# Block 0 of the experts begun in attention's last steps, the third image routed two portions a step, row loads asked a step sooner

## The chip, the cores and the metric

The kernel runs on one core of a Trainium2 chip. The core has five engines that work side by side and wait for one another by semaphores: PE (matrix products into PSUM), DVE (vector work), ACT (activations, copies), POOL (here mostly a queue that issues indirect DMAs) and SP (a queue that issues DMAs). The metric is the device time of one execution in microseconds (us); lower is better. All times below are from one execution taken by the hardware profiler, counted from its first instruction, or from the three runs listed with it.

## What is computed

Two layers over 4 images of 32 x 32 tokens with 384 channels. Each layer is a token mixer and a feed-forward part, both with a residual and a layer norm ahead of it. Only the first layer bears on the change: an attention of 12 heads, and a mixture of 4 experts of which each token uses two.

```python
attn = softmax(q @ k.T * scale)                 # per image and head, 1024 x 1024
final = row[..., :, None] * col[..., None, :]   # from a choice of the 96 best tokens per group
attn = attn * final
attn = attn / (attn.sum(axis=2, keepdims=True) + 1e-08)
x = x + (attn @ v) @ proj_w.T

probs = softmax(ln(x) @ gate_w + gate_b)        # 4 experts, the best two are kept
h = gelu(ln(x) @ w1[e] + b1[e])                 # 384 -> 1536
y = h @ w2[e] + b2[e]                           # 1536 -> 384
x = x + sum over the two experts of weight * y
```

The second layer (a local attention called outlook, and a feed-forward part called kron) follows and is not touched.

## The kernel before

**Attention** (`attention`, L177) is one loop over 202 steps. A head takes 4 steps (`PAIRS`), an image 12 heads, so heads 0 to 47 fill steps 0 to 191; ten more steps empty the pipeline. PE, DVE, ACT and SP run in the order in which the Python code records their instructions; POOL's order is set by a scheduler that reckons when each instruction could start. In step s, in this order:

- PE makes the scores of step s (L649) into two PSUM buffers `ps_s`, and ACT turns them into exponentials `e` (L659);
- PE makes the head output `ps_o` of step s - 8 (`out`, L667 with `wv`) and the sums `ps_z` of step s - 1 (`total`, L667 with ones);
- at the first step of a head, `gather` (L678) sends the sums of the head before through memory: ACT copies them to `zr`, SP writes `z_row` (L683) and reads it back as `zz` (L685);
- at the last step of a head, `keep` copies its output (L731) and puts it into the image's `q` tile: SP writes one half of the keys' partial result (L740), POOL adds the other with an accumulating DMA (L738);
- the planner fits in parts of the next image's preparation, up to 2.6 us of PE work a step (`PACE`), and the search for the best tokens (`topk`, ACT L391, DVE L395 to L431);
- DVE multiplies two `e` tiles of step s - 7 by the reciprocal sums `rz` and adds them up (`share`, L711, about 1.27 us each), and makes `wv` (L718);
- at the second step of a head, `spread` (L690) adds up `zz` (L693), and SP writes the reciprocals as `r_row` (L697) and reads them back, spread over all partitions, as `rz` (L699);
- at the end of that same second step, `Head(n + 1)` is made: eight SP loads bring the next head's rows of q and k into `q4` and `k4` (L636, L637). The scores three steps later need them.

An image's tokens are routed one image later. `routed` (L793) is a generator; the step loop takes one portion of it per step, from the 27th step of the next image on. Its portions compute the gate, choose the two experts, count and place the tokens (`Router.route`, L1313), and scatter each token's line into a table in memory with 16 indirect DMAs on POOL (L1400). After the third image, image 2, its fifteenth portion computes `router.first()` (L1408): the rows of weights and tokens for the experts' first four blocks, `NFIRST`, which need only the first three images. The fourth image is projected and routed beside the experts' first blocks (`left`, L954, handed on as `beside`).

**Experts** (`experts`, L1573) work through 35 blocks of mostly 256 tokens. For block n, POOL fetches the up and down weights (L1603), the token list `ids` (L1617) and the tokens `xb` (L1627); two sets of buffers (`halves`) alternate. DVE normalises (`norm`, L1636), PE transposes (`turn`, L1646) and DVE copies out. Then PE makes 12 portions of up products, each 3 matmuls of 128 x 256 (L1723), each followed by a GELU on ACT (L1728), and the down products (L1747 in block 0, L1767 later). In block 0, after each of its last six up portions, a portion of `beside` projects one tile of image 3 (PE L306, DVE L782, output stored by SP at L787). Block 0's weights and tokens are recorded after attention's last step, but POOL's scheduler issues them earlier, as soon as their rows and their buffers are there.

Of the kernel before, what the change touches and what calls it, by code (L numbers as in the profile page):

```python
# [17 lines left out]
P = 128  # L18
# [158 lines left out]
def attention(net, outer, router, x, x1, unsafe, qkv_wT, gpT, proj_wT, proj_w, gate_w, gate_b):  # L177
# [24 lines left out]
    with ExitStack() as ctx:  # L202

        early = ctx.enter_context(tc.tile_pool(name="at_early", bufs=1))
# [416 lines left out]
        class Head:  # L621
            def __init__(self, n):
                self.n, self.b, self.h = n, n // NH, n % NH
                self.c, self.j = self.h // 4, self.h % 4
                self.rows = slice(32 * self.j, 32 * self.j + 32)
                self.im = images[self.b]
                assert (self.b, self.c, "qk") in reached

                self.q4 = big.tile([P, 512], FP, name="q4", tag="q4", bufs=2)
                self.k4 = big.tile([P, 512], FP, name="k4", tag="k4", bufs=2)  # L630
                q = self.im["q"][self.c][self.rows, :]
                k = self.im["k"][self.c][self.rows, :].rearrange("p (a e t) -> p a e t", e=2, t=P)
                for r in range(4):
                    rows_ = slice(32 * r, 32 * r + 32)
                    odd, half = divmod(r, 2)
                    nc.sync.dma_start(out=self.q4[rows_, :], in_=q[:, 512 * half : 512 * half + 512])  # L636
                    nc.sync.dma_start(  # L637
                        out=self.k4[rows_, :].rearrange("p (a t) -> p a t", t=P), in_=k[:, :, odd, :]
                    )
                self.es = []  # L640
                self.s = tiny.tile([P, NB], FP, name="s", tag="s")
# [36 lines left out]
            def gather(self):  # L678

                zr = work.tile([P, 512], FP, name="zr", tag="zr", bufs=1)  # L680
                nc.scalar.copy(zr, self.z)
                there = rows.tile([4, 512], FP, name="z_row", tag="z_row")
                nc.sync.dma_start(out=there, in_=zr.rearrange("(j r) q -> j r q", r=32)[:, 0, :])  # L683
                self.zz = tiny.tile([P, 2, NB], FP, name="zz", tag="zz", bufs=2)
                nc.sync.dma_start(  # L685
                    out=self.zz,
                    in_=there.rearrange("j q -> (j q)").rearrange("(e p i) -> p e i", e=2, p=P),
                )
# [180 lines left out]

        step = -100  # L870
# [16 lines left out]
        heads.append(Head(0))  # L887
        goal = spent
        for step in range(STEPS + OUT + 2):
# [9 lines left out]
            if u == 0 and 0 < n <= NHEAD:  # L899
                heads[n - 1].gather()  # L900
            if 0 <= step - OUT < STEPS:
                if (step - OUT) % PAIRS == PAIRS - 1:
                    heads[(step - OUT) // PAIRS].keep()
            b, i = divmod(step, PAIRS * NH)
# [11 lines left out]
            if b and o > 2 * NB:  # L916
                next(routing[b - 1], None)
# [14 lines left out]
            if u == 1 and n + 1 < NHEAD:  # L932
                heads.append(Head(n + 1))
# [30 lines left out]
    return left  # L964
# [276 lines left out]
class Router:  # L1241
# [10 lines left out]
    def __init__(self, net, pool, keep, psum):  # L1252
# [34 lines left out]
        self.all = None  # L1287
# [285 lines left out]
def experts(net, router, x1, x2, wup, wdown, beside):  # L1573
# [12 lines left out]
    with ExitStack() as ctx:  # L1586
# [4 lines left out]
        halves = [pool(f"ex_{n}", 1) for n in range(2)]  # L1591
# [3 lines left out]
        def rows(n):  # L1595
            w, t = router.firsts if n < NFIRST else router.all
            return w[:, n : n + 1], t[:, n : n + 1]

        def weights(n):
            up = halves[n % 2].tile([P, KC * HID + NF], FP, name="up", tag="up")  # L1600
            down = halves[n % 2].tile([P, NF * C + C], FP, name="down", tag="down")
            for t, w in ((up, wup), (down, wdown)):
                nc.gpsimd.indirect_dma_start(  # L1603
                    out=t, out_offset=None, in_=w,
                    in_offset=bass.IndirectOffsetOnAxis(ap=rows(n)[0], axis=0),
                )
            return up, down

        beside = beside(work)
        ids, xbs = {}, {}  # L1610

        def tiles(n):
            return 1 if NFIRST <= n < NLEAD else TT

        def tokens(n):
            t = ids[n] = halves[0].tile([P, TT, router.LINE], I32, name="ids", tag="ids", bufs=6)
            nc.gpsimd.indirect_dma_start(  # L1617
                out=t[:, : tiles(n), :].rearrange("p t w -> p (t w)"), out_offset=None,
                in_=net.table.rearrange("(r t) w -> r (t w)", t=tiles(n)),
                in_offset=bass.IndirectOffsetOnAxis(ap=rows(n)[1], axis=0),  # L1620
            )

        def fetch(n):
            xb = xbs[n] = halves[n % 2].tile([P, TT, C], FP, name="xb", tag="xb")
            last = (B - 1 if n < NFIRST else B) * NTOK
            for t in range(tiles(n)):
                nc.gpsimd.indirect_dma_start(  # L1627
                    out=xb[:, t, :], out_offset=None, in_=x1[:last, :],
                    in_offset=bass.IndirectOffsetOnAxis(ap=ids[n][:, t, 0:1], axis=0),
                )  # L1630

        def norm(n):
            xb = xbs[n]
            own = ids.pop(n).bitcast(FP)
            for t in range(tiles(n)):
                nc.vector.tensor_scalar(  # L1636
                    xb[:, t, :], xb[:, t, :], own[:, t, 1:2], own[:, t, 2:3], ALU.subtract, ALU.mult
                )

        def turn(n):  # L1640
            xb = xbs.pop(n)
            xbT = halves[n % 2].tile([P, KC, XB], FP, name="xbT", tag="xbT")
            for t in range(tiles(n)):
                ps = router.psum()
                for c in range(KC):
                    nc.tensor.transpose(ps[:, c * P : (c + 1) * P], xb[:, t, c * P : (c + 1) * P], net.ident)  # L1646
                nc.vector.tensor_copy(
                    xbT[:, :, t * P : (t + 1) * P], ps[:, :C].rearrange("p (c t) -> p c t", c=KC)
                )
            return xbT  # L1650
# [39 lines left out]
        ws = {0: weights(0)}  # L1690
        for n in range(NFIRST):
            tokens(n)
        fetch(0)
        norm(0)
        xbT = turn(0)
        for n in range(NXB):
# [6 lines left out]
            if n + 1 < NXB:  # L1703
                if n + 1 >= NFIRST:
                    tokens(n + 1)
                ws[n + 1] = weights(n + 1)
                fetch(n + 1)
# [5 lines left out]
            up, down = ws.pop(n)  # L1713
# [5 lines left out]
            for f in (*range(0, 3), *range(6, 9), *range(3, 6), *range(9, 12)):  # L1719
                ps = ps_h.tile([P, XB], FP, name="ps_h", tag="h")[:, :size]  # L1720
                for k in range(KC):
                    o = k * HID + f * P
                    nc.tensor.matmul(  # L1723
                        ps, lhsT=up[:, o : o + P], rhs=xbT[:, k, :size], start=k == 0, stop=k == KC - 1,
                    )
                if f % 3 == 0:
                    hs[f // 3] = hp.tile([P, 3, XB], FP, name="h", tag="h")
                nc.scalar.activation(  # L1728
                    hs[f // 3][:, f % 3, :size], ps, AF.Gelu, bias=up[:, KC * HID + f : KC * HID + f + 1]
                )  # L1730
                if NFIRST <= n < NLEAD or router.all is None and n < NFIRST - 1 and (n or f % 6 >= 3):
                    next(beside, None)
                if whole and f in (8, 11):
                    g = len(ss)
                    ss.append(paired(hs[g], hs[g + 2], g))
            if n + 1 < NXB:
                norm(n + 1)
            else:
                net.scale(0, added)
            out = net.yg[first_row(n) : first_row(n + 1), :].rearrange("(p t) c -> p t c", t=tiles(n))  # L1740
            if not whole:
                for t in range(tiles(n)):
                    if t == tiles(n) - 1 and n + 1 < NXB:
                        xbT = turn(n + 1)
                    ps = ps_y.tile([P, C], FP, name="ps_y", tag="y")
                    for f in range(NF):
                        nc.tensor.matmul(  # L1747
                            ps, lhsT=hs[f // 3][:, f % 3, t * P : (t + 1) * P], rhs=down[:, f * C : (f + 1) * C],
                            start=f == 0, stop=f == NF - 1,
                        )  # L1750
                    y = work.tile([P, C], FP, name=f"y{t}", tag=f"y{t}", bufs=2)
# [31 lines left out]
            if n + 1 < NXB:  # L1783
                xbT = turn(n + 1)
# [540 lines left out]
def metaformer_kernel(  # L2325
# [57 lines left out]
    with ExitStack() as outer:  # L2383
        router = routing(outer)
        eng = mybir.EngineType
        with tc.manual_schedule(engines={eng.PE, eng.DVE, eng.Activation, eng.SP}):
            left = attention(
                net, outer, router, x, x1, unsafe, qkv_wT, gpT, proj_wT, proj_w, gate_w, gate_b
            )
            done = experts(net, router, x1, x2, wup, wdown, left)  # L2390
# [75 lines left out]
```

## Time and profile before

| | us |
| --- | --- |
| three runs | 2771.51, 2778.27, 2787.73 (median 2778.27) |
| the profiled execution | 2779.0 |
| its span, first to last instruction | 2776.9 |
| PE busy | 2563.9 (92%) |
| DVE busy | 1746.2 (63%) |
| ACT busy | 1272.1 (46%) |
| POOL busy | 414.5 (15%) |
| last scores of attention start | 1194.7 |
| last `ps_o` of attention ends | 1226.5 |
| first up product of block 0 starts | 1229.6 |
| first up product of block 1 starts | 1279.7 |

From 200 to 300 us PE is busy 98.1 us of 100 and DVE 76.9; from 1158.7 to 1188.8, PE 17.9 of 30.1; from 1203.7 to 1226.6, PE 12.7 of 22.9 at a granted clock of 0.55, DVE 18.6. A line of the timeline holds the start, the duration of all that it merges, the engine, the source line, the operation, output and inputs, a count, and in brackets the idle time before it and what ended that. SPq stands for the queue of SP. "Slices" are fortieths of the span, 69.4 us each.

### The profile page before, as it was taken

The page shows a single profiled execution, that of the slowest core. Times are in us where ns is not written, and L with a number is a line of the kernel's source. Part 1 is how long each engine was busy: PE and PEld are TensorE (multiplying, and loading weights), DVE is VectorE, ACT ScalarE, POOL GpSimd, SP SyncE. Part 2 cuts the span into 40 slices and gives each one's busy share as a digit, 9 for nine tenths or more (in the row PEclk, how much of TensorE's full clock was granted, in tenths as well). Part 3 has the DMA queues.
Part 4 walks back from the last instruction along what each step waited for, and adds up shares of the span by engine and source line. Part 5 has one row for each costly group of instructions (what it writes and reads, how often), then busy time and mean ns, then how long its engine had stood idle before and what let it go on. Part 6 is the DMA issues. An engine that isn't in the chain of part 4 may idle for free. (4 is left out here: it accounts for less than half of the span.)

```text
span 2776.9 us, 40200 instructions
## 1 busy us (share of the span) xinstructions
PE 2563.9 (92%) x14667; PEld 1555.7 (56%) x14667; DVE 1746.2 (63%) x4490; ACT 1272.1 (46%) x2086; POOL 414.5 (15%) x501
## 2 busy tenths in 40 slices
PE   6879998989898999679999999999999998999988
PEld 3323332333332332137889999999999974555542
DVE  2367768777776778555635444455465457897962
ACT  3768776667676777421121211211211123445455
POOL 1000000020003000412221111222222111110000
PEclk9989999989998999779999999999999999999999
DMA  5133334322331233445475455556656626765532
GB/s 108 33 98 91 103 91 124 104 56 63 92 78 46 70 87 85 130 128 190 158 280 207 181 187 207 213 208 222 228 195 223 225 100 220 213 213 180 174 117 93
DMA packets 215807, 404.13 MB, mean 146 GB/s; under 512 B 83345, under 2 KB 176849, under 8 KB 202545
## 3 DMA queue, kind: packets, MB, share of 16 engines
q0 software_dynamic: 26960, 209.05, 21.9%
q1 hardware_dynamic: 178928, 181.52, 21.8%
q10 hardware_dynamic: 9712, 10.91, 1.3%
q8 instruction: 118, 1.93, 0.3%
q14 instruction: 89, 0.72, 0.1%
HBM read 304.34 MB, written 49.00 MB: 127 GB/s over the span
## 5 line engine op out<-in xcount | busy, mean ns | idle before, releaser
L1728 ACT ACTIVATE h<-ps_h,up 128x256 f32<-128x256 f32 (+1 forms) x420 | 194.9, 465 | 835.2 <-PE ps_h L1723 818.6
L1723 PE MATMUL ps_h<-xbT,up 128*128 128x256 f32 (+1 forms) x2520 | 531.2, 371 | 2.5 <-ACT h L1728 1.4
L1723 PEld LDWEIGHTS ps_h<-xbT,up 128*128 128x128 f32 x2520 | 462.4, 191 | 64.9 <-ACT h L1728 2.2
L711 DVE CUSTOM_DVE_ANT_0 e<-e,rz,inv 128x1024 f32<-128x1024 f32 x384 | 475.2, 1274 | 35.7 <-DMA rz<-r_row 35.7
L659 ACT ACTIVATE e<-ps_s,ten 128x1024 f32<-128x1024 f32 x384 | 407.6, 1107 | 96.5 <-PE ps_s L649 41.6
L649 PE MATMUL ps_s<-q,k 32*128 32x512 f32 x1536 | 291.3, 669 | 66.1 <-ACT e L659 32.7
L667 PE MATMUL ps_o<-e,wv 128*32 128x512 f32 x1536 | 229.0, 671 | 47.6 <-DVE wv L718 30.2
L738 POOL DMA_DIRECT2D q<-po x96 | 76.0, 874 | 977.9 <-DMA q<-po 651.1
L667 PE MATMUL ps_z<-e,rt_ones 128*32 128x512 f32 x1536 | 219.7, 646 | 0.0
L391 ACT ACTIVATE below<-tk_left,tk_bound 128x1024 bf16<-128x1024 f32 (+1 forms) x160 | 184.2, 1151 | 70.6 <-DVE tk_bound L397 60.1
L1767 PE MATMUL ps_y<-wsum,hsum 128*128 128x192 f32 x1116 | 197.1, 330 | 9.9 <-DVE hsum L1683 5.4
L649 PEld LDWEIGHTS ps_s<-q,k 32*128 32x128 f32 x1536 | 89.4, 191 | 203.2 <-issue 89.3
L1767 PEld LDWEIGHTS ps_y<-wsum,hsum 128*128 128x128 f32 x1116 | 183.3, 192 | 13.7 <-DVE y L1771 7.4
L1907 PE MATMUL ps_a<-wa,xnT 128*128 128x486 f32 x384 | 162.4, 572 | 1.8 <-ACT xnT L174 1.8
L1771 DVE TENSOR_TENSOR y<-ps_y,y 128x192 f32<-128x192 f32 x155 | 55.4, 357 | 167.8 <-PE ps_y L1767 162.0
L667 PEld LDWEIGHTS ps_o<-e,wv 128*32 128x32 f32 x1536 | 31.7, 112 | 209.0 <-issue 83.5
L306 PE MATMUL ps_t<-xnT,wqkv 128*128 128x512 f32 x288 | 136.9, 616 | 3.3 <-ACT xnT L488 2.6
L1567 POOL DMA_INDIRECT yt<-yg,index x64 | 78.0, 1218 | 358.8 <-DVE x L1870 164.7
L667 PEld LDWEIGHTS ps_z<-e,rt_ones 128*32 128x32 f32 x1536 | 52.8, 118 | 132.7 <-issue 129.7
L1767 PE MATMUL ps_y<-down,h 128*128 128x192 f32 x744 | 126.0, 326 | 0.0
L1767 PEld LDWEIGHTS ps_y<-down,h 128*128 128x128 f32 x744 | 122.6, 190 | 1.6
L1907 PEld LDWEIGHTS ps_a<-wa,xnT 128*128 128x128 f32 x384 | 71.2, 189 | 74.2 <-issue 70.2
(403 smaller groups left out, 3588.1 us busy)
## 6 DMA issues: line engine op xcount, KB each, us to landing
band<-room SPq DMA_DIRECT2D x32, 1560.0 KB
rz<-r_row SPq DMA_DIRECT2D x48, 512.0 KB
yg<-y SPq DMA_DIRECT2D x67, 192.0 KB
q<-q SPq DMA_DIRECT2D x192, 64.0 KB
k<-k SPq DMA_DIRECT2D x192, 64.0 KB
room<-none SPq DMA_DIRECT2D x64, 192.0 KB
x<-x SPq DMA_DIRECT2D x34, 192.0 KB
o<-in_x_dram SPq DMA_DIRECT2D x33, 192.0 KB
```

Of the source, the lines that this page charges most:

```text
L306: nc.tensor.matmul(ps, lhsT=lhsT(k), rhs=rhs(k), start=k == 0, stop=k == KC - 1)
L391: nc.scalar.activation(junk[:n], left[:n], AF.Sign, bias=bound[:n], accum_out=over[:n])
L649: nc.tensor.matmul(ps[:, half * 512 : half * 512 + 512], lhsT=self.k4[r, u * P : (u + 1) * P], rhs=self.q4[r, :], start=True, stop=True,)
L659: nc.scalar.activation(e, ps, AF.Exp, bias=shift, scale=QK_SCALE)
L667: nc.tensor.matmul(ps[r : r + 32, :], lhsT=lhsT(odd), rhs=self.es[2 * u + odd][:, half * 512 : half * 512 + 512], start=u == 0, stop=u == ...
L711: nc.vector.tensor_tensor_reduce(self.es[m], self.es[m], self.rz, 1.0, self.im["inv"][:, m, self.h : self.h + 1], ALU.mult, ALU.add, self. ...
L738: nc.gpsimd.dma_start(out=there, in_=po[r : r + 32, :], accum_op=ALU.add)
L1567: self.nc.gpsimd.indirect_dma_start(out=y, out_offset=None, in_=self.net.yg[: first_row(self.complete(i // NB)), :], in_offset=bass.Indire ...
L1723: nc.tensor.matmul(ps, lhsT=up[:, o : o + P], rhs=xbT[:, k, :size], start=k == 0, stop=k == KC - 1,)
L1728: nc.scalar.activation(hs[f // 3][:, f % 3, :size], ps, AF.Gelu, bias=up[:, KC * HID + f : KC * HID + f + 1])
L1767: nc.tensor.matmul(ps, lhsT=left[f], rhs=right[:, f, :], start=f == 0, stop=f == HF - 1)
L1907: nc.tensor.matmul(pa[:, :HW_], lhsT=xnTs[i][:, k, :], rhs=wa[:, k, hh * HW_ : (hh + 1) * HW_], start=k == 0, stop=k == KC - 1,)
```

## The change

There are four parts.

1. `Head(n + 1)` is made at the first step of head n instead of the end of its second, and its loads become a generator, `load`. `gather` issues three of the eight between its two own DMAs; the rest follow it in the same step, ahead of `spread`'s.
2. Of image 2 the loop takes two routing portions a step.
3. As soon as `router.first()` has run, the pool of attention's early tiles (weights, the image's transposed tokens, moved to the other side of the memory for it) is closed, and the first half's buffers of the experts take its place. Block 0's up weights and the token lists of four blocks are asked for in that step, its tokens one step later, its down weights three steps after those; its norm stands in step 188 and its transposes in step 189, copied out by ACT instead of DVE. In steps 192 to 199 its 12 up portions are made, by turns one and two a step, into the score buffers, and the GELU results go into three free `q` tiles.
4. In `experts`, block 0 then starts at its down products. The six portions of `beside` that stood between its up products stand after every fourth down portion. The helpers of `experts` become the methods of a class `Blocks`, the same for all later blocks. The norm of block 1 is recorded after block 0's up portions as before, which now means ahead of all six portions of `beside`.

```diff
-        early = ctx.enter_context(tc.tile_pool(name="at_early", bufs=1))
+        soon = ctx.enter_context(ExitStack())
+        early = soon.enter_context(tc.tile_pool(name="at_early", bufs=1, side="right"))
...
+            def load(self):
...
                     nc.sync.dma_start(out=self.q4[rows_, :], in_=q[:, 512 * half : 512 * half + 512])
+                    yield
                     nc.sync.dma_start(
                         out=self.k4[rows_, :].rearrange("p (a t) -> p a t", t=P), in_=k[:, :, odd, :]
                     )
+                    yield
...
-            def gather(self):
+            def gather(self, loads):
...
                 nc.sync.dma_start(out=there, in_=zr.rearrange("(j r) q -> j r q", r=32)[:, 0, :])
+                for _ in range(3):
+                    next(loads, None)
...
+        def chunks():
+
+            cols, h = [], None
+            for f in range(NF):
+                if f % 4 == 0:
+                    h = lasting.tile([P, NTOK], FP, name="q", tag="q", bufs=6)
+                if f % 2 == 0:
+                    ps = ps_s.tile([P, NTOK], FP, name="ps_s", tag="s")
+                p = ps[:, f % 2 * 512 : f % 2 * 512 + XB]
+                blocks.up(0, f, blocks.xbT, p, XB)
+                col = h[:, f % 4 * XB : f % 4 * XB + XB]
+                blocks.gelu(0, f, p, col)
+                cols.append(col)
+                yield
+            blocks.cols = cols
...
-            if u == 0 and 0 < n <= NHEAD:
-                heads[n - 1].gather()
+            if u == 0 and n <= NHEAD:
+                loads = iter(())
+                if n + 1 < NHEAD:
+                    heads.append(Head(n + 1))
+                    loads = heads[-1].load()
+                if n:
+                    heads[n - 1].gather(loads)
+                for _ in loads:
+                    pass
...
+            if step >= STEPS:
+                if step == STEPS:
+                    upward = chunks()
+                for _ in range(1 + step % 2):
+                    next(upward, None)
...
-                next(routing[b - 1], None)
+                for _ in range(2 if b == B - 1 else 1):
+                    next(routing[b - 1], None)
+            if blocks is None and router.firsts is not None:
+                assert pending == [None, None] and begun == len(tiles)
+                soon.close()
+                pool = outer.enter_context(tc.tile_pool(name="ex_0", bufs=1, side="right", reuse_waits="tile"))
+                blocks = Blocks(net, router, x1, wup, wdown, pool)
+                known = step
+                blocks.weigh(0, 0)
+                for one in range(NFIRST):
+                    blocks.tokens(one)
+            if blocks and step == known + 1:
+                blocks.fetch(0)
+            if blocks and step == known + 4:
+                blocks.weigh(0, 1)
+            if step == STEPS - 4:
+                blocks.norm(0)
+            if step == STEPS - 3:
+                blocks.xbT = blocks.turn(0, nc.scalar.copy)
...
-            if u == 1 and n + 1 < NHEAD:
-                heads.append(Head(n + 1))
...
+            early = n == 0 and blocks.cols is not None
-            for f in (*range(0, 3), *range(6, 9), *range(3, 6), *range(9, 12)):
+            for f in () if early else (*range(0, 3), *range(6, 9), *range(3, 6), *range(9, 12)):
...
             if n + 1 < NXB:
-                norm(n + 1)
+                blocks.norm(n + 1)
...
                     for f in range(NF):
+                        h = blocks.cols[f] if early else hs[f // 3][:, f % 3, :]
                         nc.tensor.matmul(
-                            ps, lhsT=hs[f // 3][:, f % 3, t * P : (t + 1) * P], rhs=down[:, f * C : (f + 1) * C],
+                            ps, lhsT=h[:, t * P : (t + 1) * P], rhs=down[:, f * C : (f + 1) * C],
                             start=f == 0, stop=f == NF - 1,
                         )
+                        if early and f % 4 == 3:
+                            next(beside, None)
```

The new methods that the step loop calls:

```python
def weigh(self, n, part):
    name, w = (("up", self.wup), ("down", self.wdown))[part]
    t = self.halves[n % 2].tile([P, w.shape[-1]], FP, name=name, tag=name)
    self.ws.setdefault(n, []).append(t)
    self.nc.gpsimd.indirect_dma_start(
        out=t, out_offset=None, in_=w,
        in_offset=bass.IndirectOffsetOnAxis(ap=self.rows(n)[0], axis=0),
    )
def up(self, n, f, xbT, ps, size):
    up = self.ws[n][0]
    for k in range(KC):
        o = k * HID + f * P
        self.nc.tensor.matmul(
            ps, lhsT=up[:, o : o + P], rhs=xbT[:, k, :size], start=k == 0, stop=k == KC - 1,
        )
def gelu(self, n, f, ps, out):
    up = self.ws[n][0]
    self.nc.scalar.activation(out, ps, AF.Gelu, bias=up[:, KC * HID + f : KC * HID + f + 1])
```

## The prediction

> **What bounds the kernel now.** I first read the busy shares by slice, which show where PE stops being full, then PE's timeline over that place, then SP's and POOL's timelines over the same stretch, and last the list of waits from 60 to 1240 us, for the part of the change that touches every head. Times are us in the profiled execution.
>
> ```profile
> PE   6879998989898999679999999999999998999988
> PEclk9989999989998999779999999999999999999999
> ```
>
> PE (and its granted clock) is at 9 tenths almost everywhere, except in slices 17 and 18, 1111 to 1250 us: attention's last steps and the start of the experts. Work moved into that hole is nearly free; work moved elsewhere is not.
>
> ```profile
> 1167.38 1.04 PE L667 MATMUL ps_z<-e,rt_ones 128*32 128x512 f32 x8
> 1180.11 4.37 PE L649 MATMUL ps_s<-q,k 32*128 32x512 f32 x8 [11.69 <-DMA q<-q]
> ...
> 1224.59 1.94 PE L667 MATMUL ps_o<-e,wv 128*32 128x512 f32 x8 [1.00 <-DVE wv L718]
> ...
> 1229.62 11.16 PE L1723 MATMUL ps_h<-xbT,up 128*128 128x256 f32 x42 [0.65 <-DVE xbT L1647]
> 1240.63 2.12 PE L306 MATMUL ps_t<-wproj,q 128*128 128x388 f32 x6
> ...
> 1279.68 1.46 PE L1723 MATMUL ps_h<-xbT,up 128*128 128x256 f32 x6
> ```
>
> PE's timeline has three parts. One stall of 11.7 us waits for the last head's row loads. Then a tail, to 1226.5, waits for DVE (wv) at every step. Then block 0: from the last out, 1226.53, to the first up product of block 1, 1279.68, are 53.2 us.
>
> ```profile
> 1163.23 0.32 SPq L697 DMA_DIRECT2D r_row<-rr  x1
> 1173.92 0.32 SPq L699 DMA_DIRECT2D rz<-r_row  x1
> 1174.33 0.55 SPq L636 DMA_DIRECT2D q<-q  x1
> ```
>
> SP's queue tells the stall's cause. rz is issued only when r_row has landed, normally 1.4 us later; here 10.7 us. The row loads stand behind it.
>
> ```profile
> 1160.32 1.96 POOL L1603 DMA_INDIRECT up<-in_wup_dram,rows_w_first  x1 [0.30 <-issue]
> 1162.58 0.97 POOL L1603 DMA_INDIRECT down<-in_wdown_dram,rows_w_first  x1 [0.30 <-issue]
> ...
> 1177.44 0.94 POOL L1627 DMA_INDIRECT xb<-x,ids  x1 [8.52 <-DMA ids<-table,rows_t_first]
> ```
>
> POOL had just asked for block 0's weights: 128 x 4620 and 128 x 4992 floats, 2.37 + 2.56 = 4.92 MB. A 4 KB row issued into that burst landed at its end, and so did ids. 4.92 MB in the 11.6 us from 1162.3 to 1173.9 is 424 GB/s: 5.6 us for up, 6.0 for down.
>
> ```profile
> DVE e L711 <- DMA rz<-r_row: 35.7, 15, 13.2
> DVE zall L693 <- DMA zz<-z_row: 35.4, 19, 4.1
> PE ps_s L649 <- DMA k<-k: 11.0, 10, 4.2
> ```
>
> The waits (total, times, longest) show what the earlier row loads touch: 11.0 us of PE waiting for k rows can go; DVE's waits for zz and rz can grow.
>
> **A, the row loads a step sooner.** No load is added; eight per head move in SP's order. Now: z_row, zz (median 1.7 us after z_row, when it has landed), r_row (at +3.85 when DVE is prompt), rz (+5.3), then eight loads of 0.52 to 0.65 us. After: z_row, three loads, zz, five loads, r_row, rz. Three loads and z_row's own 0.53 make zz +2.4, 0.7 later. With zz's 0.4 and five loads r_row comes no sooner than +6.2, up to 2.35 later. I set this against each head's own slack, the start of its first share (DVE L711) less rz's landing, taken as issue + 3.8, as in the two last heads, where DVE waited for it. Over the 46 heads that load rows behind them the excess is 22 us of new DVE waiting, in 21 heads; zz adds 0.7 at each of its 19 waits, 13 more. PE mostly takes a wv some time after it is ready (0 to 4.7 us; under 1 us in two heads of five). Taking that margin off head by head leaves 8 to 9 us of the 22, and I take 4 of the 13: a loss of 12. The gain: 11.0 us of PE waits go, and the half-speed restarts after the two longest of them (4.45 and 3.50 us for eight rows against 2.3) give 3 more: 14. A = -2, with ends -14 (every delay covered) and +21 (all 35 lost, 14 gained). The order of the next image's preparation shifts by a step in some places, with the same instructions; its cover is the planner's spread, and I price it at nothing.
>
> **B, image 2 (the third) routed two portions a step.** The fifteenth portion, which gives block 0's rows, falls in step 178 instead of 185. Its DVE work moves (matmul portion 3.0, copies 0.4, rows 5.1, from 1120.9 to 1124.0 and 1153.8 to 1159.0) and is not added: DVE is busy 18 of 20 us around 1100, so steps 171 to 178 lengthen by about what 179 to 185 lose. The 16 scatters (POOL L1400, 1.27 us each, 25 us with their stretches) start near step 176 instead of 181. In the changed program's POOL order up, four ids, down follow them directly: although the source asks for down four steps later, nothing it waits for holds it back. So the burst stays about 12 us, near steps 180 to 183 of head 44's chain, and up and down are split only by five issues (some 6 us). What is late next is z_row, zz, r_row or rz of that head: four transfers in turn, each at most one half (6 us) late, needed some 11.5 us after z_row. The last head's rows are by then not behind rz. I count 6.5 us of new stall for the 13.2 now at 1166, plus a slow restart less (4.37 against 2.3): about -7.5. Ends: -16, if the burst falls between two chains, and -2, if it hits two links fully.
>
> The Trainium skill speaks against this picture: "DMA: Bandwidth & Descriptors", section Queues, rings and completion order, has each DMA engine alternate between queues packet by packet, so a small SP transfer should get its turn inside POOL's burst. The 10.7 us row says it waited for the whole of it. By the rule alone the stall would not be this burst's, nothing of the 7.5 would be gained, and the forecast would be about 7 us higher; the row decides.
>
> **C, block 0's up products in the tail.** Moved: 36 up matmuls (72 rows, 15.70 us in a later block, 1.31 for each of 12 portions), 12 GELUs of 465 ns and their table load (1.28). In steps 192 to 199 DVE works 2.94 us a step (two L711, d, wv), which sets the pace; PE's out is 1.06 at full clock, and 1 or 2 portions add 1.3 or 2.6, 3.0 a step on average: covered, but only at full clock (granted now: 0.55), which the added work itself should bring. If it doesn't, PE sets the pace, 5.8 a step. DVE's norm of block 0 (0.87) and PE's six transposes with ACT's two copies (0.9 and about 1.1) go into steps 188 and 189, where PE is nearly full: D = +1.5, ends 0 and +3.
>
> From the last out (t = 0), PE does: two portions, 2.6; four down portions, 8 of 24 rows of 7.90, to 5.2; project 0 needs head 47's rows in q: ACT's copy 0.6, SP's issue 0.6, POOL's accumulate 2.0 behind that (1180.6 + 0.6 to 1183.2 for head 44), 0.8 to issue and 2 to land: 6, so project 0 ends at 8.1; four portions, 10.7; project 1, 12.8; four portions, 15.5. Project 2 needs the PSUM buffer of project 0, emptied by a DVE add that now stands behind DVE's norm of block 1. That needs xb of block 1, which in POOL's order stands behind up of block 2, up and down of block 1: 7.28 MB, 17.2 us from about 5, then 0.4 MB and its landing: 24. Norm 0.87 and add 0.7: 25.5. Project 2 at a cold clock 3.0; transposes with their waits 1.5; three times four portions and a project, 14.2: block 1 begins near 44. 53.2 - 44 = 9 gained, of 15.7 + 3.4 that left. Ends: -19 (xb in time, no stall) and -5 (accumulated rows and x loads late too). Weights of block 1 land near 22: covered by 22 us.
>
> **Sum.** Profiled time 2779.0 (span 2776.9 and 2.1 around it; the runs' median is 2778.27). -2 - 7.5 - 9 + 1.5 = -17: 2762.
>
> **Rivals.** (1) The burst misses head chains and xb lands in time: 2779 - 2 - 16 - 19 + 1.5 = 2743.5. For it: the burst is shorter than a head's 21 us; against: the FIFO-like wait of ids (8.52) at 1177. (2) The stall only moves: B -2, C -5, A 0, D +1.5 gives 2773.5. For it: down follows up directly, and xb follows 7.28 MB; against: the last rows no longer wait behind rz. (3) Slower: r_row behind five loads in 46 heads, the full 35 us in DVE's path with the k waits replaced by it: 2779 + 35 - 7.5 - 9 + 1.5 = 2799. It decides once A costs more than 15 + 14 = 29. For it: slack under 0.8 in twenty of the 46 heads; against: PE is busy 90 of 100 us from 100 to 1085, DVE 72, so part of a DVE wait is always covered.
>
> **How the numbers follow.** Chances: the likeliest (2754 to 2770) 0.45, rival 1 0.22, rival 2 0.22, rival 3 0.11. The range reaches into both sides: 2742 to 2788. Half a per cent, 13.9 us, is about what the measurement can tell from no change, so faster means under 2764.4: rival 1, two thirds of the likeliest and a little of rival 2, 0.54; slower means over 2792, 0.11; the rest 0.35.
>
> **What would show it.** A: k-row waits of PE near nothing; the zz and rz waits of DVE grown by 10 to 35. B: up issued near 1135, no wait of 11 us before the last head's scores, but a DVE wait of 3 to 9 for zz or rz one head after the burst begins. C: L1723's successor in the tail at a clock near 1, DVE shares still 2.94 apart, then one PE wait of about 10 us before project 2, behind DVE's norm of block 1, and 44 us from last out to block 1. Wrong would be: shares further apart than 3.1, DVE waiting at block 0's norm for xb, or a main part (100 to 1085) longer by over 15 us.

## The result, and the profile after

| | before | after |
| --- | --- | --- |
| median of 6 runs each, us | 2777.74 | 2813.36 (2809.45 to 2818.41) |
| ratio | 1 | 1.0143, 95% interval 1.0121 to 1.0166 |
| span of the profiled execution, us | 2776.9 | 2813.9 |

The change made the kernel slower, by 36 us between the medians and 37 between the profiled spans; the interval is 1.2 to 1.7%. The forecast was 2762 and its range ended at 2788. The third rival (slower, 2799) named the mechanism and was still 14 us short.

The busy shares of PE by slice, of the changed kernel (a slice is now 70.3 us):

```profile
PE   6879898889998998687999999999999998999988
```

The hole, now in slices 17 to 19, is still there. But slices 5 to 16, attention's main part, have digits that add up to 102 where they added up to 104: the loss is spread thin, and a page of slices hardly shows it. The starts of single instructions do. How much later than in the profile before a head's `z_row` is issued by SP, and what follows attention:

| place | head 6 | 12 | 18 | 24 | 36 | 42 | 44 | 46 | last out ends | block 1 starts | block 4 starts | end |
| --- | --- | --- | --- | --- | --- | --- | --- | --- | --- | --- | --- | --- |
| later by, us | 8.1 | 15.0 | 21.1 | 26.3 | 26.9 | 38.8 | 58.9 | 38.9 | 40.9 | 36.1 | 37.6 | 37.0 |

By head 41 (37.4), before image 2's routing and block 0's weights come into play, the whole loss is there. It doesn't grow evenly: from head 24 to head 37 it stays between 21 and 27. Image 2's routing costs 20 and gives 20 back; the tail and block 0 give back a few.

The waits of the changed kernel from 60 to 1240 us (total, times, longest):

```profile
DVE e L719 <- DMA rz<-r_row: 78.1, 32, 5.7
DVE zall L701 <- DMA zz<-z_row: 59.1, 28, 4.2
```

PE's waits for k rows are gone from the list, as forecast (step A's gain came). The waits for rz and zz have grown from 35.7 and 35.4 to 78.1 and 59.1: by 66, not by the 35 that A allowed at most. SP's queue shows why. One head (33) before, then after:

```profile
902.49 0.54 SPq L683 DMA_DIRECT2D z_row<-zr  x1
904.21 0.37 SPq L685 DMA_DIRECT2D zz<-z_row  x1
906.90 0.33 SPq L697 DMA_DIRECT2D r_row<-rr  x1
908.31 0.32 SPq L699 DMA_DIRECT2D rz<-r_row  x1
```

```profile
923.42 0.54 SPq L689 DMA_DIRECT2D z_row<-zr  x1
...
925.95 0.59 SPq L693 DMA_DIRECT2D zz<-z_row  x1
926.58 0.63 SPq L644 DMA_DIRECT2D k<-k  x1
...
929.21 0.63 SPq L644 DMA_DIRECT2D k<-k  x1
929.95 0.53 SPq L705 DMA_DIRECT2D r_row<-rr  x1
931.58 0.33 SPq L707 DMA_DIRECT2D rz<-r_row  x1
```

r_row goes out 6.5 us after z_row instead of 4.4, and rz 8.2 instead of 5.8. This is one of the better heads: over heads 0 to 45 the medians after z_row are 2.55 (zz), 7.88 (r_row) and 9.91 (rz), against 1.72, 4.38 and 6.09 in a second profile of the kernel before, taken below (e0). In 33 of the 46 heads the first share starts within 0.6 us of rz's landing (its issue + 3.8); in e0 it is 15. The row loads have turned the chain z_row, zz, r_row, rz from a frequent limit into the usual one.

The tail and block 0, from PE's timeline of the changed kernel, and the DVE instruction that the long wait stands for:

```profile
1266.40 1.06 PE L673 MATMUL ps_o<-e,wv 128*32 128x512 f32 x8
...
1274.34 2.12 PE L307 MATMUL ps_t<-wproj,q 128*128 128x388 f32 x6
...
1278.87 2.12 PE L307 MATMUL ps_t<-wproj,q 128*128 128x388 f32 x6
...
1296.33 4.22 PE L307 MATMUL ps_t<-wproj,q 128*128 128x388 f32 x6 [12.76 <-DVE gate_o L791]
...
1315.73 1.46 PE L1711 MATMUL ps_h<-xbT,up 128*128 128x256 f32 x6
```

```profile
1294.69 0.96 DVE L1683 TENSOR_SCALAR xb<-xb,ids 128x384 f32<-128x384 f32 x2 [23.12 <-DMA xb<-x,ids]
```

Two projections run at once; the third waits 12.8 us because DVE stands at block 1's norm, which waits 23 us for xb. The forecast was 10, with the same cause. From the last out to block 1 it takes 48.3 us (forecast 44).

### The profile page after: what moved, and what is told of

Same layout as the page of the kernel before. It is cut to its first block, busy times and chain, and to the rows that moved or that the text cites. A ratio compares the mean times of both kernels' runs of the same rounds, so it can differ in the third digit from the quotient of the medians.

```text
span 2813.9 us, 40158 instructions
## 1 busy us (share of the span) xinstructions
PE 2566.9 (91%) x14667; PEld 1553.0 (55%) x14667; DVE 1746.1 (62%) x4488; ACT 1275.0 (45%) x2088; POOL 411.7 (15%) x501
## 3 DMA queue, kind: packets, MB, share of 16 engines
q8 instruction: 118, 1.93, 0.3%
## 5 line engine op out<-in xcount | busy, mean ns | idle before, releaser
L1711 PE MATMUL ps_h<-xbT,up 128*128 128x256 f32 (+1 forms) x2448 | 512.7, 370 | 2.4 <-ACT h L1717 2.4
L1711 PEld LDWEIGHTS ps_h<-xbT,up 128*128 128x128 f32 x2448 | 447.5, 190 | 61.0 <-ACT h L1717 3.6
L655 PE MATMUL ps_s<-q,k 32*128 32x512 f32 x1536 | 284.0, 682 | 50.2 <-ACT e L665 44.1
```

What stands on the lines that cost most here:

```text
L655: nc.tensor.matmul(ps[:, half * 512 : half * 512 + 512], lhsT=self.k4[r, u * P : (u + 1) * P], rhs=self.q4[r, :], start=True, stop=True,)
L1711: self.nc.tensor.matmul(ps, lhsT=up[:, o : o + P], rhs=xbT[:, k, :size], start=k == 0, stop=k == KC - 1,)
```

## The experiments

e1 to e4 ran on one chip, e0 and e6 to e8 on a second, e5, e10 and e11 on a third, each group with the kernel before beside it. The chips differ (before: 2748.87 on the first, 2778 on the two others), so ratios are compared. "Loads" are a head's eight row loads.

**e1: the loads put back**, all else as changed.

```diff
-                loads = iter(())
-                if n + 1 < NHEAD:
-                    heads.append(Head(n + 1))
-                    loads = heads[-1].load()
...
             search()
+            if u == 1 and n + 1 < NHEAD:
+                heads.append(Head(n + 1))
+                for _ in heads[-1].load():
+                    pass
```

> The changed kernel with the eight row loads put back behind rz, where the kernel before has them; the earlier block, the double routing and the up products in the tail stay. Theory A (SP's order: r_row and rz stand behind the loads in every head): the 37 us that the steps up to 172 lost come back and the 5 us won behind the last out stay, about 2772, between 2766 and 2780, and r_row is again 3.8 us after z_row. Rival (the main part is longer because of something else in the change, such as the pools' new places or the burst): still above 2800.

Measured: ratio 1.0020 (1.0007 to 1.0033), 5.5 us (1.9 to 9.1) above the kernel before. The main part's loss is gone: r_row's median is 4.29 again, and DVE's waits (60 to 1240 us) are near those of the kernel before:

```profile
DVE zall L701 <- DMA zz<-z_row: 41.5, 21, 3.8
DVE e L719 <- DMA rz<-r_row: 33.2, 16, 9.1
```

But with the three other parts of the change, forecast at -15 together, the kernel is not faster than before, and the ratio lies just above the expected range (2780 beside 2778 is 1.001).

**e2: the loads alone**, in the kernel before: the same edit as in the change, nothing of its other parts.

> The kernel before with the row loads alone asked a step sooner, as in the changed kernel. Theory A: slower by 30 to 42, 2808 to 2820, less some 10 if the last head's 11.7 us wait for its rows goes with it. Rival (something else in the change): within 8 of the kernel before.

Measured: 1.0139 (1.0122 to 1.0156), 38 us (34 to 43). The waits are those of the changed kernel, and more:

```profile
DVE e L718 <- DMA rz<-r_row: 93.3, 34, 15.3
DVE zall L700 <- DMA zz<-z_row: 59.7, 32, 4.3
```

One part of the change, by itself, is as slow as the whole. e1 and e2 together show that the loads' place in SP's queue is the cause of the loss, and exclude the pools and the burst as its cause.

**e3 and e4: which link?** e3 issues three loads between z_row and zz and five behind rz. e4 issues none ahead of zz and eight between zz and r_row.

```diff
                     heads[n - 1].gather(loads)
-                for _ in loads:
-                    pass
...
             search()
+            if u == 1:
+                for _ in loads:
+                    pass
```

The first edit is e3's, the second, in `gather`, e4's.

```diff
-                for _ in range(3):
-                    next(loads, None)
                 self.zz = tiny.tile([P, 2, NB], FP, name="zz", tag="zz", bufs=2)
```

> The changed kernel with three loads between z_row and zz, and five behind rz: zz is 0.7 to 0.9 us late as in the changed kernel, r_row is late only by that. If the delay of r_row and rz is what costs: 4 to 10 above the kernel with all loads put back, so 2776 to 2784. If the delay of zz costs as much, or if it is that rows are moved while z_row lands: above 2795.

> The changed kernel with no load ahead of zz, and all eight between zz and r_row: zz is prompt (1.7 us after z_row), r_row comes no sooner than 1.7 + 0.5 + 8 x 0.64 = 7.3 us after z_row, 8.6 with the two room stores. If the delay of r_row and rz is what costs: 2810 to 2825, as slow as the changed kernel or slower. If the delay of zz is what costs: below 2790.

Measured: e3 1.0051 (1.0034 to 1.0068), 6.6 us above e1; e4 1.0260 (1.0237 to 1.0283), 64 above e1 and well beyond the changed kernel. The waits of e3, then of e4 (60 to 1240 us):

```profile
DVE zall L701 <- DMA zz<-z_row: 69.9, 31, 4.3
DVE e L719 <- DMA rz<-r_row: 39.4, 21, 8.2
PE ps_s L655 <- DMA k<-k: 5.7, 2, 5.1
```

```profile
DVE e L717 <- DMA rz<-r_row: 130.5, 36, 13.3
DVE zall L699 <- DMA zz<-z_row: 35.9, 22, 3.6
```

In e3 zz is 0.9 later (median 2.61), rz only by that, and DVE waits for zz 28 us longer than in e1 (41.5); PE's k waits shrink from 19.4 to 5.7, and the sum of it is small. In e4 zz is prompt, rz goes out at 10.72, and DVE waits 97 us longer for it than in e1 (33.2). A delay that begins behind zz is enough to cost this much (e4); e3 costs less because its whole chain is only 0.9 late.

**e5: the room stores.** Attention's steps also issue stores (L85, `room`, 0.64 us each) between the loads and r_row; step A had left them out.

```diff
-            if zeros and step >= 4:
-                zeros.pop(0)()
...
                 heads[n - 1].spread()
+            if zeros and step >= 4:
+                zeros.pop(0)()
```

> The changed kernel with each step's two room stores (L85) issued behind r_row and rz instead of ahead of them; the loads stay a step sooner. If the prediction's r_row time (no sooner than +6.2) was missed mainly because two room stores of 0.64 us stand behind the five loads in the heads up to about 19: r_row 1.3 us sooner in those heads, and 8 to 20 us of the 38 come back: 1.007 to 1.011 of before. Rival (the loads alone do it, room is hidden): within 5 of the changed kernel, 1.0125 to 1.016.

Measured: 1.0133 (1.0114 to 1.0152), not told apart from the changed kernel. The edit did less than expected: SP's timeline shows that one of the two stores still stands ahead of r_row, whose median only fell from 7.88 to 7.17. So the omission explains part of why +6.2 was too early, but 0.7 of r_row's lateness bought no time that can be told apart. What both stores would bring wasn't tried.

**e0: the kernel before again**, for a second profile beside the next three.

> The kernel before, unchanged, for a profile on the same chip as the next three. Expected: the wait of 11 to 12 us for a row before the last heads' scores, and 49 to 53 us from the last out to block 1, wherever the chip's own time lies.

Measured: 2777.69, its span 2775.6. PE's list of waits from 60 to 1240 us:

```profile
PE ps_s L649 <- DMA k<-k: 20.4, 7, 11.8
```

The long wait is there again (11.8). But block 1 starts 48.8 us after the last out, not 53.2: in the profile on record DVE waited 8.3 us for one x row block (1.6 here), PE then waited 2.8 for DVE's norm of block 1, and 24 rows of down products after it took 9.6 instead of 7.9. This execution, e2 and e7 (48.8, 48.8, 48.7) have none of this.

**e6: the loads earlier still**, for head n + 2 at the end of head n's fourth step, when their buffers come free, ahead of z_row.

```diff
+            if u == PAIRS - 1 and n + 2 < NHEAD:
+                heads.append(Head(n + 2))
+                for _ in heads[-1].load():
+                    pass
```

> The changed kernel with the eight loads of head n+2 asked at the end of head n's fourth step, as soon as their buffers are free and ahead of the next z_row. Theory A: zz, r_row and rz are prompt again, PE's waits for k rows (11 us before) go too: 5 to 12 faster than the changed kernel with the loads put back, so 0.995 to 1.000 of the kernel before. Rival (SP's queue is simply full there: the loads wait for the scores and z_row comes behind 5.2 us of issue): z_row late by 1 to 3 in every head, 1.01 or more.

Measured: 1.0060 (1.0041 to 1.0078): slower, the rival's way, though less than its 1.01. ACT's copy, then SP's queue:

```profile
709.00 0.60 ACT L687 COPY zr<-ps_z 128x512 f32<-128x512 f32 x1
```

```profile
709.17 0.63 SPq L644 DMA_DIRECT2D k<-k  x1
709.91 0.54 SPq L689 DMA_DIRECT2D z_row<-zr  x1
```

zr was ready at 709.60, z_row went out at 709.91 behind the last load. On average over 48 heads z_row is issued 1.62 us after zr is ready; in e0 it is 0.06. The queue must be empty at the moment when z_row, zz, r_row and rz become ready, and here it isn't.

**e7: the double routing alone**, in the kernel before.

```diff
             if b and o > 2 * NB:
-                next(routing[b - 1], None)
+                for _ in range(2 if b == B - 1 else 1):
+                    next(routing[b - 1], None)
```

> The kernel before with the third image routed two portions a step, nothing else. By step B of the prediction: 2 to 16 faster, likeliest 7.5 (0.997). Rival (the burst meets another head's rows and DVE is full there): the burst starts some 35 us sooner, a wait of 8 to 12 for rows or rz stands there in place of the 11.7, and the time stays within 4 of before, or is above it.

Measured: 0.9979 (0.9958 to 1.0000), 5.8 us below before, 0 to 11.7. Against e0, z_row of heads 43, 44, 45 and 46 stands at +8.2, +15.7, +9.2 and -2.8, and the last out ends 2.7 sooner. The routing is moved, not saved; POOL asks for the weights at 1131.3 to 1133.5, between two heads' chains, and the 11.8 us wait for rows is gone from the list (the longest wait for zz in that stretch is 5.1). Yet at the last out only a quarter of it is left as a gain. ACT stands for 3.6, 1.8 and 3.0 us between 1129 and 1158 for no instruction or transfer that the profile names; what these are wasn't settled.

**e8: block 1's norm later**, e1 with norm and transposes of block 1 at the end of block 0's down portions.

```diff
-                blocks.norm(n + 1)
+                if not early:
+                    blocks.norm(n + 1)
...
                     for f in range(NF):
+                        if early and t == tiles(n) - 1 and f == 8:
+                            blocks.norm(n + 1)
...
+                if early:
+                    xbT = blocks.turn(n + 1)
```

> The changed kernel with the loads put back, and block 1's norm and transposes moved from the middle of block 0's down portions to their end. Theory (project 2 waits only because DVE stands at that norm for xb): the wait of 12.4 goes, block 1 starts 34 to 37 after the last out instead of 47, and the time is 10 to 13 below the kernel with the loads put back: 0.997 to 0.999 of before. Rival (the weights or x loads of block 1 come as late as xb): PE waits at block 1's first product instead, less than 4 gained.

Measured: 0.9973 (0.9959 to 0.9987), 7.5 below before. The wait before project 2 is gone, and block 1 starts 41.5 us after the last out (e1: 46.9), not 34 to 37. DVE's timeline shows the next limit, and SP's when the late transfer was asked for:

```profile
1253.26 0.55 DVE L790 TENSOR_TENSOR o<-o,ps_t 128x384 f32<-128x384 f32 x1 [12.11 <-DMA o<-in_x_dram]
```

```profile
1234.81 0.44 SPq L772 DMA_DIRECT2D o<-in_x_dram  x1
```

An x row block (192 KB) asked at 1234.81, 2 us after the last of three weight requests (1229.23 to 1232.76, 7.28 MB), was there at 1253.3; the profile's DMA records hold rows of these weights from 1231.5 to 1252.5. By the ratios e8 is 13 us below e1, as expected, but from the last out to block 4 it saves only 6; e1 ran on another chip, and the rest isn't explained.

**e10: the x rows ahead of the burst**, e8 with the seven o loads issued at the first projection, into seven buffers.

```diff
-                o = late[0].tile([P, C], FP, name="o", tag="o", bufs=2)
+                o = late[0].tile([P, C], FP, name="o", tag="o", bufs=7)
...
-            if t + 1 < NB:
-                residue(B - 1, t + 1)
+            for soon_ in range(1, NB) if t == 0 else ():
+                residue(B - 1, soon_)
```

> The kernel with the loads put back and block 1's norm moved to the end, and all seven remaining loads of x rows (o) asked at the first projection, into seven buffers instead of two. Theory (in that kernel DVE's 12.1 us wait for one o, asked 2 us behind the 7.28 MB of weights, has taken the place of the wait for xb): no DVE wait above 3 us between the last out and block 1, block 1 starts 35 to 38 after the last out instead of 41.5, 3 to 6 faster: about 0.995 of before. Rival (the o loads only push the weights or xb back by as much): block 1 or its norm waits instead, within 2 of that kernel, 0.997.

Measured: 0.9949 (0.9933 to 0.9965), 14 us below the kernel before: this version beats both kernels. Three DVE waits for o of 4.6 to 5.9 remain, more than expected, but PE doesn't see them. Its timeline from the last projection of block 0 to block 1:

```profile
1258.62 2.12 PE L307 MATMUL ps_t<-wproj,q 128*128 128x388 f32 x6
1261.74 0.52 PE L1691 MATMUL ps_t<-ident,xb 128*128 128x128 f32 x3 [1.00 <-DVE xb L1681]
1262.67 0.52 PE L1691 MATMUL ps_t<-ident,xb 128*128 128x128 f32 x3 [0.41 <-DVE gate_o L791]
1264.68 1.56 PE L1709 MATMUL ps_h<-xbT,up 128*128 128x256 f32 x6 [1.50 <-DVE xbT L1694]
```

1264.68 is 35.6 us after the last out (1229.07), within the 35 to 38 expected.

**e11: two loads in each landing gap**, e10 with two loads between z_row and zz, two between r_row and rz, and four behind rz.

> As the kernel with the x rows asked ahead, with two row loads (1.3 us) in the 1.7 us in which SP waits for z_row to land, two in the 1.4 us in which it waits for r_row to land, and four behind rz. Theory A (only a load that makes zz, r_row or rz later costs): zz and r_row at most 0.2 later, rz 0.2, the last load 2.5 us sooner, k waits of PE smaller: between 5 faster and 2 slower than the kernel without it. Rival (any load asked between z_row and rz slows the chain, by its traffic): 5 or more slower.

Measured: 0.9960 (0.9945 to 0.9975), not told apart from e10: the mean is 2.9 us higher, with an interval of -1.5 to 7.2, so the rival's 5 isn't excluded by the time. zz is 0.2 later (median 1.95), r_row and rz 0.2 and 0.5, which is little; DVE's waits for zz and rz grow from 71.9 to 98.8 all the same, and PE's k waits shrink from e10's 14.8 to 5.5. Filling the gaps brings nothing, but costs far less than asking the loads a step sooner.

## Why the prediction was wrong

| part | forecast (ends) | measured, us |
| --- | --- | --- |
| A, the loads a step sooner | -2 (-14, +21) | +38 (+34 to +43), e2 |
| B, two portions a step | -7.5 (-16, -2) | -5.8 (-11.7 to 0), e7; -2.7 at the last out |
| C, up products in the tail | -9 (-19, -5) | about 0: block 4 starts 153.1 after the last out in e0, 153.0 in e2, 153.5 in e1 (on e2's chip), 155.2 in the changed kernel |
| D, norm and transposes in steps 188, 189 | +1.5 (0, +3) | +2.3 between two single executions: last out at 1224.8 in e8, 1222.5 in e7; not settled, since e10, the same up to there, has 1229.1 on another chip |

B, C and D so measured add up to -3.5, but e1, which has all three, is 5.5 slower than the kernel before. The 9 us between them aren't explained; no profile of the kernel before was taken on e1's chip.

**A is the step that failed, in size: -2 was forecast, +38 measured.** The mechanism was written down: r_row and rz behind five loads, DVE waiting for rz. Its price was wrong three times over. The prediction's own sign of being wrong, a main part longer by over 15 us, came.

- "r_row comes no sooner than +6.2" was taken as the place where r_row would be. It was a floor, and its own terms (2.4, 0.4 and five loads of 0.52 to 0.65) give only 5.4 to 6.05. Measured were +6.5 in the best heads and 7.88 in the median. In head 33 zz went out at +2.5, the next load 0.63 later instead of 0.4, and the five loads took 0.67 each with their gaps. The room stores were forgotten, and in heads where r_row had been late the delay came on top of that lateness; I had let it vanish in it. rz also followed r_row 1.6 us later instead of 1.4 in head 33.
- So "22 us of new DVE waiting" and 13 for zz, 35 in all, became 66.
- "Taking that margin off head by head leaves 8 to 9 us of the 22, and I take 4 of the 13": 12 of 35 were to reach the end. Measured: e2 lost 38 and had gained what PE no longer waited for k rows (20.4 in e0, 2.2 left), so that the loss alone was near 56, of the 81 by which its waits for rz and zz (93.3 and 59.7) exceed e0's (35.4 and 36.6): seven tenths, not a third. e2 and e0 ran on different chips; reckoned in the same way against e1, on e2's chip, it is six tenths in e3 and nearly nine in e4. Why the margins covered so little isn't shown. A reading: a margin between a ready wv and PE's use of it is a lead that PE can fall back on once, and a delay in every head uses it up in the first ones. The 21 us lost by head 18 fit it, the flat stretch from head 24 to 37 doesn't; no run isolated it.

The upper end of A, +21, fell with the same 35. The third rival priced the same delay at 35 too, and gave it 0.11 because part of a DVE wait "is always covered"; it should have had the chance that the 33 heads at their limit show.

**B was right in sign and within its ends.** Its terms as written (13.2 less 6.5, and 2.1 for the restart) give -8.8 rather than -7.5. The 11.7 us wait went; the up request came at 1170.7 in the changed kernel, not near 1135, mostly because everything was later (e7: 1131.3). In the head behind the burst DVE waited 3.3 for zz and 2.7 for rz, no longer than in many other heads; in e7 it waited 5.1 for zz.

**C's mechanism was right, its base wrong.** The one long PE wait before project 2, behind DVE's norm of block 1, came as forecast (12.8 for 10; the rows of the 7.28 MB ran from 6.8 us after the last out for 19.5 us, where 5 and 17.2 were taken), and PE's granted clock in the tail was 1.00 from 1245 to 1271 where it had been 0.55. But the 53.2 that it was taken from was one execution's; the usual is 48.8. Of 48.8, 46.9 to 48.3 remained, and block 1 itself took longer (e1: 38.7 against 35.8 in e0). What left the hole was paid back by one wait: 15.7 us of products had been covering the eight projections and the transfers, and moved away they left these bare. e8 and e10 show how much was there: block 4 starts 147.2 and 140.9 after the last out, 6 and 12 sooner than in e0.

**The skill's rule.** The Trainium skill, "DMA: Bandwidth & Descriptors", section Queues, rings and completion order, has each DMA engine alternate between queues packet by packet. The prediction set this against the row of 10.7 us and let the row decide. The profile's DMA records show that there was nothing to decide: the row and the rule agree. From 1167 to 1173.5 us of the profile before, POOL's queue (q0) and SP's (q1) moved (packets, MB, share of the 16 engines):

```profile
q0 software_dynamic: 159, 2.78, 100.2%
q1 hardware_dynamic: 144, 0.00, 1.2%
```

128 of the 144 are r_row's, of 32 bytes each, and they took turns with weight rows of 18 to 20 KB (0.75 us for a row of the down weights). r_row's packets ran from 3.8 to 9.5 us after its issue; in head 33, with no burst, from 0.8 to 1.0 us after it. So r_row was late because its many short packets each took a turn beside long ones, not because it stood behind the whole burst, as the prediction read it: r_row was complete at 1173.4, and the last weight row ended at 1176.4. By these rows the burst ran at 366 GB/s (4.92 MB from 1163.0 to 1176.4), not at 424. In e8 it was the same: from 1239 to 1250 us 223 weight rows and 225 packets of x rows moved, and the late o load stood in its queue behind a store of x.

## What to carry to other kernels

An issue queue is a resource like an engine: a load that is asked early costs nothing only if no later link of a latency chain stands behind it in the same queue. Look at when each link becomes ready and keep the queue empty there; between the same loads behind the chain and in the gaps where it waits for a landing no difference could be told (e10, e11), a step sooner they cost 38 us. A delay repeated in every iteration can't be written off against margins found in single iterations: of the waiting that it caused here, six to nine tenths reached the end, where a third had been taken. The term that is repeated 46 times deserves more care than three that happen once.

When work leaves a stretch, ask what it was covering: here the products hid a norm's data and the x rows, and only moving the norm behind the projections and asking the x rows before the weights made the move pay.

## What the runs showed of the hardware

- The kernel before, at the same time of 2778, had 53.2 us from the last out to block 1 in one profile and 48.8 in another; a single profiled execution may hold a stall of 4 us that others don't.
- Chips differ by 1%: the kernel before took 2748.9 on one and 2778 on the others.
- A transfer of 4 KB in 128 packets of 32 bytes, asked beside rows of 18 to 20 KB, had its last packet 9.5 us after its issue, and 1.0 us after it when nothing else ran.
- While POOL issues its 16 scatters and the weights, engines stop for times that the profile ascribes to nothing, up to 9.0 us on ACT in the changed kernel (before e at 1170.96). The profile lists two queues that fetch instructions (1.93 and 0.72 MB in the whole span). The Trainium skill, "Runtime: NRT & Kernel Launch", section Instruction fetch mechanics, has engines refill their instructions by DMA in blocks of 16 KiB, mostly hidden. The packets of these two queues are here almost all of 16,384 and 8,192 bytes, and none is recorded between 1157.7 and 1186.5 us, so the records show no refill in that stop; its cause stays open.
